# A list scheduler that knows the 64-column form of TensorE matmuls: a four-layer graph network on one NeuronCore

## Chip, cores and metric

The kernel runs on one core of a Trainium2 chip. The metric is the device time of one execution, in microseconds (us). The core has five engines with one instruction queue each: PE (TensorE, matrix multiplication), DVE (VectorE), ACT (ScalarE), POOL (GpSimd) and SP (here it only starts DMA transfers). An engine takes the instructions of its queue in their order; the engines wait for one another by semaphores. PE writes into PSUM, which has eight banks of 512 fp32 values per partition; DVE and ACT read the results from there.

## What is computed

The input is a batch of 64 graphs with 256 nodes and 256 features each, and a 0/1 adjacency matrix per graph. Four residual layers follow one another:

```python
h = relu(layernorm(x)); x = x + gat4(h, adj)        # layer 0: 4 heads of 64, softmax over neighbours, elu
h = relu(layernorm(x)); x = x + relation4(h, adj)   # layer 1: 4 heads of 64, softmax, relu, layernorm per head
h = relu(layernorm(x)); x = x + gat1(h, adj)        # layer 2: 1 head of 256
h = relu(layernorm(x)); x = x + gru3(h, adj)        # layer 3: 3 rounds of h = GRU(A^T (h W_i), h)
```

Layers 0 and 1 end in a product of attention weights and features per head: `alpha[256,256] @ Wh[256,64]`. Layer 3 has, in every round, an aggregation over neighbours and a GRU cell with gates r, z and n.

## The kernel before

**Units.** The graphs are handled in 33 units: one graph, 31 pairs, one graph. `graphs(u, first, nb)` writes down, for one unit, all operations of the four layers (`layer0`, `layer1`, `layer2`, `gru`). It does not run them: every `op(engine, cost, emit, reads, writes, takes)` makes an `_Op` with an estimated cost in ns, and its dependences are taken from the buffers that it reads and writes.

**The scheduler.** `_Schedule.run` then plays the whole program through a simple model of five engines while the kernel is being built, and issues the instructions in the order in which the model starts them. Every operation has a due time, reckoned back from the end that is planned for its unit (one pair per `PACE` = 104000 ns). When an engine of the model falls free, it takes from its heap `able[e]` the operation with the earliest due time whose buffers are to be had (`roomy`). Costs thus do not only describe: **the model's clock decides the order of all five queues, and which slot of a pool (`bank0` to `bank7`, `g0` to `g8` and so on) a buffer gets**, since the free slot with the lowest number is taken when an operation starts. About three units are in flight at a time, so that the matrix products of one unit's GRU stand between the attention of another.

**The 64-column form.** `attend_heads` makes one PE operation out of two heads. Each of its products uses only 64 columns of the array at a time (in the profile: `128*64 128x65`, line 1163); all other products in these layers use all 128. For a pair of graphs the operation has 64 matmuls as the profile counts them. Before the change its cost is

```python
op("pe", pe(944) * len(hs) + 90, emit, [*pts, wh], banks_, takes=[o])
```

that is 1978 ns for two heads of a pair, wherever it stands.

**Names that the prediction uses.** All `vec(...)` calls are recorded by one helper, so they carry line 829; they are told apart by tiles.

- L1163 `bank<-wh,pt`: the attention products (64 columns in layers 0 and 1; full width in layer 2). `pt` are the weights that DVE makes (L1145, and L829 `pt<-pt,cap`). DVE empties the banks by `rs<-bank` (a reciprocal) and `o<-bank,rs`.
- L1032 `bank<-ident,xn`: transposes of the normalised input; ACT copies them by `ht<-bank`.
- L1389 `bank<-ident,ht`: transposes of the new GRU state, in two blocks of 4 matmuls, one for each half `j` of the features. The state's halves are made by the last of a row of DVE operations (`g<-g,ht`, `g<-g,g`, then `ht<-g,g`), which follow ACT's tanh of gate z (`g<-bank,bg`) and of gate n (`g<-g,bg`). From the transposes ACT and DVE make `hl`, the state split into two parts.
- L1361 `bank<-am_r,hl`: the aggregation over neighbours; ACT copies its two banks by `ag<-bank`.
- L1375: the GRU gates, 4 matmuls each: `bank<-ht,whh` needs only the state, `bank<-ag,wc` needs `ag`.
- L1308 `xt<-xt,o` adds the result of layer 1 to `x`; L997 and L998 are statistics of a layer norm, L1006 and L1007 its power on POOL, L1015 its application on ACT.

Of the kernel before, what the change touches and what calls it, by code (L numbers as in the profile page):

```python
# [538 lines left out]
class _Op:  # L539
    __slots__ = (  # L540
        "engine", "cost", "port", "emit", "group", "bufs", "takes", "nbytes", "succs", "waits", "due", "ready",
        "index",
    )


class _Schedule:
# [14 lines left out]
    DMA_RATE = 220.0  # L561
    DMA_AHEAD = 2000
    STRETCH = 3.13
    MARGIN = 800.0

    def __init__(self, tc, pools):
# [8 lines left out]
    def buf(self, cls, shape, dtype=F32, tile=None):  # L575
        return _Buf(cls, shape, dtype, tile)

    def op(self, engine, cost, emit, reads=(), writes=(), takes=(), nbytes=0, port=False):
        o = _Op()
        o.port = port  # L580
        o.engine, o.cost, o.emit, o.group, o.nbytes = engine, cost, emit, self.group, nbytes
        o.succs, o.index, o.ready = [], len(self.ops), 0.0
        deps, o.bufs, o.takes = set(), [], []
        for written, items in ((False, reads), (True, writes)):
            for item in items:
                b, part = item if isinstance(item, tuple) else (item, None)
                if b not in o.bufs:
                    o.bufs.append(b)
                    b.left += 1
                if written and b.tile is None and b not in o.takes:  # L590
                    o.takes.append(b)
                keys = list(b.parts) if part is None else [k for k in (part, None) if k in b.parts]
                for k in keys:
                    writer, readers = b.parts[k]
                    if writer is not None:
                        deps.add(writer)
                    if written:
                        deps.update(readers)
                writer, readers = b.parts.get(part, (None, []))
                if written:  # L600
                    if part is None:
                        b.parts.clear()
                    b.parts[part] = (o.index, [])
                else:
                    b.parts[part] = (writer, readers + [o.index])
        for b in takes:
            if b.tile is None and b not in o.takes:
                o.takes.append(b)
        deps.discard(o.index)
        o.waits = len(deps)  # L610
        for d in deps:
            self.ops[d].succs.append(o)
        self.ops.append(o)
        return o
# [17 lines left out]
                )  # L632
            self.last[i.engine] = i.name

    def enable(self, ops, able):
        for o in ops:
            o.waits -= 1
            if o.waits == 0:
                heapq.heappush(able[o.engine], (o.due, o.index))

    def roomy(self, o):
        need = {}
        for b in o.takes:
            if b.tile is None:
                need[b.cls] = need.get(b.cls, 0) + 1
        return all(len(self.free[c]) >= n for c, n in need.items())
# [9 lines left out]
    def run(self):  # L656
        ops = self.ops
        for o in reversed(ops):
            late = self.end[o.group]
            for s in o.succs:  # L660
                if s.group == o.group or o.group not in self.end or o.group < 0:
                    late = min(late, s.due - self.STRETCH * s.cost - self.MARGIN)
            if o.nbytes:
                late -= self.DMA_LATENCY + o.nbytes / self.DMA_RATE
            o.due = late
        engines = ("pe", "act", "dve", "pool", "sp")
        able = {e: [] for e in engines}
        idle = dict.fromkeys(engines, True)
        events = []
        clock = self.dma_free = self.port_free = 0.0  # L670
        count = 0

        def post(t, kind, o):
            nonlocal count
            count += 1
            heapq.heappush(events, (t, count, kind, o))

        for o in ops:
            if o.waits == 0:
                heapq.heappush(able[o.engine], (o.due, o.index))  # L680
        done = 0
        self.trace = []
        while True:
            for e in engines:
                if not idle[e]:
                    continue
                if e == "sp" and self.dma_free > clock + self.DMA_AHEAD:
                    continue
                held = []
                while able[e]:  # L690
                    item = heapq.heappop(able[e])
                    o = ops[item[1]]
                    if (not o.port or self.port_free <= clock) and self.roomy(o):
                        self.start(o, clock)
                        idle[e] = False
                        free = clock + o.cost - self.OVERLAP[e]
                        post(free, "free", o)
                        if o.port:
                            self.port_free = free
                        break  # L700
                    held.append(item)
                for item in held:
                    heapq.heappush(able[e], item)
            if not events:
                break
            clock = events[0][0]
            while events and events[0][0] == clock:
                _, _, kind, o = heapq.heappop(events)
                if kind == "free":
                    idle[o.engine] = True  # L710
                    if o.nbytes:
                        self.dma_free = max(self.dma_free, clock) + o.nbytes / self.DMA_RATE
                        post(self.dma_free + self.DMA_LATENCY, "done", o)
                        post(max(clock, self.dma_free - self.DMA_AHEAD), "dma", o)
                    else:
                        post(clock + self.OVERLAP[o.engine] + self.HOP[o.engine], "done", o)
                    if o.engine == "pe":
                        self.enable([s for s in o.succs if s.engine == "pe"], able)
                elif kind == "done":
                    done += 1  # L720
                    self.enable([s for s in o.succs if s.engine != "pe" or o.engine != "pe"], able)
                    for b in o.bufs:
                        b.left -= 1
                        if b.left == 0 and b.slot is not None:
                            heapq.heappush(self.free[b.cls], b.slot)
        self.span = clock
        assert done == len(ops), [o.index for o in ops if o.waits][:5]
# [3 lines left out]
def _fast_path(  # L731
# [88 lines left out]
    buf, op = sched.buf, sched.op  # L820
# [4 lines left out]
    def bank(dtype=F32):  # L825
        return buf("bank", [P, S * 4 // mybir.dt.size(dtype)], dtype)
# [149 lines left out]
    def graphs(u, first, nb):  # L976
# [5 lines left out]
        def part_of(fixed):  # L982
            return lambda cost: fixed + (cost - fixed) * nb / 2

        pe, act, dve, pool = part_of(0), part_of(200), part_of(130), part_of(130)
# [172 lines left out]
        def attend(ps, pt, wh, c, h, w, Q):  # L1158
            b, ic = divmod(c, 2)
            for jc in range(2):  # L1160
                for q in range(P // Q):
                    i0 = ic * P + q * Q
                    nc.tensor.matmul(  # L1163
                        ps[q * Q : (q + 1) * Q], lhsT=pt.tile[:, b, jc, i0 : i0 + Q],
                        rhs=wh.tile[:, h, 2 * b + jc, :w], start=(jc == 0), stop=(jc == 1),
                    )

        def attend_heads(o, o_view, pts, wh, hs):

            banks_ = [bank() for _ in hs]  # L1170
            w = E + 1

            def emit():
                for ps, pt, h in zip(banks_, pts, hs):
                    for c in range(C):
                        attend(ps.tile[:, c * w : (c + 1) * w], pt, wh, c, h, w, P // 2)

            op("pe", pe(944) * len(hs) + 90, emit, [*pts, wh], banks_, takes=[o])

            def scaled(ps, h):  # L1180
                rs = buf("rs", [P, C])
                view = lambda: ps.tile[:, : C * w].rearrange("p (c w) -> p c w", c=C)
                vec(nc.vector.reciprocal, 175, lambda: rs.tile, lambda: view()[:, :, E], reads=[ps], writes=[rs])
                vec(nc.vector.tensor_mul, dve(420), lambda: o_view(h), lambda: view()[:, :, :E],
                    lambda: rs.tile[:, :, None].to_broadcast([P, C, E]), reads=[ps, rs], writes=[(o, h)])

            for ps, h in zip(banks_, hs):
                scaled(ps, h)
# [345 lines left out]
```

## Time and profile before

| | |
|---|---|
| median of 3 executions | 3197.43 us (3197.04 to 3197.90) |
| the profiled execution, first to last instruction | 3198.1 us, 0.7 us above that median; nothing outside this span is shown |
| PE busy | 3143.2 us (98%), 18599 matmuls |
| DVE busy | 2321.4 us (73%) |
| ACT busy | 1486.8 us (46%) |
| POOL busy | 897.4 us (28%) |
| DMA | 43 GB/s on average |
| granted PE clock | 0.996 |
| L1163 with 64 columns | 8192 matmuls, 263.7 us busy |

From about 390 us to 2810 us the work repeats itself with every pair: the same order of instructions, one period per pair. Before that the pipeline fills, after it the last units run out. Busy times are sums over an engine's instructions; matmuls are pipelined and their ends are modelled, so the start of the following group is the safer measure of how long a group held PE.

### The profile page before, as it was taken

What the parts mean: (1) busy time and instruction counts of PE and PEld (TensorE: products, weight loads), DVE (VectorE), ACT (ScalarE), POOL (GpSimd) and SP (SyncE); (2) the same over time, 40 slices, a digit from 0 to 9 for tenths busy, and PEclk for the clock granted to TensorE, in tenths of its full rate; (3) what the DMA queues carried; (4) which work ended last, traced back from release to release, by engine and by line L of the source; (5) the groups of instructions that cost most, each with busy time, mean ns of one, the idle gap of its engine ahead of it and who ended that gap; (6) DMA issues with size and microseconds to landing.
All of it is one profiled execution on the core that took longest, in us unless ns stands there. A gap on an engine that the chain in (4) does not pass through costs nothing.

```text
span 3198.1 us, 48707 instructions
## 1 busy us (share of the span) xinstructions
PE 3143.2 (98%) x18599; PEld 1931.9 (60%) x18599; DVE 2321.4 (73%) x5206; ACT 1486.8 (46%) x3128; POOL 897.4 (28%) x907
## 2 busy tenths in 40 slices
PE   7899999999999999999999999999999999999998
PEld 6765656565666655566656566556566556665555
DVE  7777867778767778767678677788677787677753
ACT  5454444454454444454444454544444444544433
POOL 4323332133331233331233321333311333311210
PEclk9999999999999999999999999999999999999999
DMA  4110111101111101111101111111111011101000
GB/s 129 34 49 29 54 54 34 47 31 50 54 54 34 47 31 50 54 47 34 53 28 54 53 36 45 40 41 54 54 34 47 31 50 50 47 23 44 11 16 12
DMA packets 109927, 138.82 MB, mean 43 GB/s; under 512 B 44714, under 2 KB 97524, under 8 KB 102004
## 3 DMA queue, kind: packets, MB, share of 16 engines
q1 hardware_dynamic: 105712, 134.25, 12.8%
q8 instruction: 149, 2.44, 0.3%
q10 hardware_dynamic: 3972, 1.36, 0.2%
q14 instruction: 94, 0.77, 0.1%
HBM read 109.84 MB, written 17.34 MB: 40 GB/s over the span
## 4 chain that ended last, share of the span: by engine, by line
PE 87%; DVE 9%; POOL 2%; ACT 1%; issue 1%; DMA 0%; SPq 0%; ACTq 0%; POOLq 0%; DVEq 0%
PE bank L1375 55%; PE bank L1054 10%; PE bank L1163 10%; PE bank L1361 5%; PE bank L1032 3%; PE bank L1389 2%; DVE pt L1145 2%; DVE g L829 2%; DVE pt L829 1%; POOL mean L1297 1%; POOL o L829 1%; DVE o L829 1%; ACT ht L829 1%; DVE xt L1308 1%; DVE mean L829 1%
## 5 line engine op out<-in xcount | busy, mean ns | idle before, releaser
L1375 PE MATMUL bank<-ag,wc 128*128 128x512 f32 (+1 forms) x2376 | 1063.0, 582 | 0.0
L1375 PE MATMUL bank<-ht,whh 128*128 128x512 f32 (+1 forms) x2376 | 1055.6, 580 | 2.2 <-ACT g L829 1.3
L829 ACT ACTIVATE g<-bank,bg 128x512 f32<-128x512 f32 (+1 forms) x594 | 395.2, 670 | 713.6 <-PE bank L1375 706.6
L1375 PEld LDWEIGHTS bank<-ag,wc 128*128 128x128 f32 x2376 | 441.4, 190 | 459.2 <-issue 441.1
L1375 PEld LDWEIGHTS bank<-ht,whh 128*128 128x128 f32 x2376 | 435.0, 190 | 438.9 <-issue 424.2
L1006 POOL TENSOR_SCALAR mv<-mv 128x4 f32<-128x4 f32 (+1 forms) x132 | 81.9, 621 | 1428.6 <-DVE mv L998 1383.6
L1145 DVE TENSOR_SCALAR pt<-cb,f 128x256 f32<-128x256 f32 x1152 | 416.9, 430 | 6.0 <-ACT cb L1099 5.2
L1163 PEld LDWEIGHTS bank<-wh,pt 128*64 128x64 f32 (+1 forms) x8704 | 345.6, 142 | 94.4 <-issue 76.1
L829 DVE SCALAR_TENSOR_TENSOR g<-g,g 128x512 f32<-128x512 f32 (+1 forms) x396 | 263.3, 670 | 180.4 <-ACT g L829 180.4
L1163 PE MATMUL bank<-wh,pt 128*64 128x65 f32 (+1 forms) x8704 | 382.0, 233 | 9.7 <-DVE pt L829 5.8
L829 DVE TENSOR_TENSOR pt<-pt,cap 128x1024 f32<-128x1024 f32 (+1 forms) x297 | 341.3, 1193 | 0.1
L829 DVE SCALAR_TENSOR_TENSOR g<-bank,g 128x512 f32<-128x512 f32 (+1 forms) x198 | 129.8, 666 | 280.2 <-PE bank L1375 280.0
L829 DVE SCALAR_TENSOR_TENSOR g<-g,ht 128x512 f32<-128x512 f32 (+1 forms) x198 | 136.5, 689 | 172.0 <-ACT g L829 171.6
L1361 PE MATMUL bank<-am_r,hl 128*128 128x256 f32 x1536 | 238.1, 304 | 0.1
L1015 ACT ACTIVATE xn<-xt,mv 128x256 f32<-128x256 f32 x384 | 197.3, 588 | 72.1 <-DVE mv L829 71.9
L1361 PEld LDWEIGHTS bank<-am_r,hl 128*128 128x128 f32 x1536 | 198.2, 189 | 42.5 <-issue 30.6
L829 ACT COPY ag<-bank 128x512 f32<-128x512 f32 (+1 forms) x198 | 113.4, 573 | 233.4 <-PE bank L1361 230.1
L829 ACT ACTIVATE g<-g,bg 128x512 f32<-128x512 f32 (+1 forms) x198 | 137.6, 709 | 161.6 <-DVE g L829 159.4
L997 DVE BATCH_NORM_STATS2 st<-xt 128x6 f32<-128x256 f32 x512 | 208.1, 406 | 6.4 <-DMA xt<-in_x_dram 6.2
L829 ACT COPY ht<-bank 128x512 f32<-128x512 f32 (+1 forms) x264 | 137.8, 573 | 124.0 <-PE bank L1032 123.8
L1136 POOL MEMSET wh<- 128x16 f32 (+3 forms) x99 | 11.8, 120 | 635.5 <-ACT f L1130 635.5
L1007 POOL TENSOR_TENSOR mv<-mv,nhalf 128x4 f32<-128x4 f32 (+1 forms) x132 | 176.0, 1333 | 11.0
(91 smaller groups left out, 3452.2 us busy)
## 6 DMA issues: line engine op xcount, KB each, us to landing
cb<-rd SPq DMA_DIRECT2D x60, 1024.0 KB
xt<-in_x_dram SPq DMA_DIRECT2D x31, 512.0 KB
at<-in_adj_dram SPq DMA_DIRECT2D x31, 512.0 KB
out_dram<-xt SPq DMA_DIRECT2D x31, 512.0 KB
cb<-rd SPq DMA_DIRECT2D x30, 256.0 KB
cap<-cap_n SPq DMA_TRANSPOSE x128
cb<-rd SPq DMA_DIRECT2D x2, 512.0 KB
rd<-row ACTq DMA_DIRECT2D x60, 8.0 KB
```

Of the source, the lines that this page charges most:

```text
L829: emit = lambda: fn(*[a() if callable(a) else a for a in args], **kw)
L997: nc.vector.bn_stats(st.tile[:, c, :], xt.tile[:, c, :])
L1006: nc.gpsimd.tensor_scalar(mv.tile[:, 2, :], mv.tile[:, 1, :], 1e-5, None, op0=OP.add)
L1007: nc.gpsimd.tensor_tensor(mv.tile[:, 2, :], mv.tile[:, 2, :], nhalf[:, :C], op=OP.pow)
L1015: op("act", 610, lambda: nc.scalar.activation(xn.tile[:, c, :], xt.tile[:, c, :], AF.Relu, bias=mv.tile[:, 3, c : c + 1], scale=mv.tile[:, ...
L1032: nc.tensor.transpose(ps.tile[:, c * P : (c + 1) * P], xn.tile[:, c, dc * P : (dc + 1) * P], ident)
L1054: nc.tensor.matmul(ps.tile[:, : heads * W], lhsT=ht.tile[:, dc, c * P : (c + 1) * P], rhs=we[:, dc].rearrange("p h w -> p (h w)"), start=( ...
L1145: nc.vector.tensor_scalar(pt.tile[:, b, jc, :].rearrange("p (i n) -> p i n", n=P), cb.tile[:, h, 2 * b : 2 * b + 2, :], f.tile[:, 1, h, c ...
L1163: nc.tensor.matmul(ps[q * Q : (q + 1) * Q], lhsT=pt.tile[:, b, jc, i0 : i0 + Q], rhs=wh.tile[:, h, 2 * b + jc, :w], start=(jc == 0), stop= ...
L1361: nc.tensor.matmul(ps.tile[:, b * N : (b + 1) * N], lhsT=hl.tile[:, k, 2 * b + sc, :], rhs=am.tile[:, 2 * b + sc, :], start=(k == 0 and sc ...
L1375: nc.tensor.matmul(ps.tile[:, :S], lhsT=w[:, dc, g * P : (g + 1) * P], rhs=v.tile[:, dc, :], start=(first and dc == 0), stop=(last and dc ...
L1389: nc.tensor.transpose(ps.tile[:, c * P : (c + 1) * P], ht.tile[:, j, c * P : (c + 1) * P], ident)
```

## The change

Three things are new in the scheduler, and one line in the kernel.

1. An `_Op` may be `tiled`. Only the operation of `attend_heads` is. Its cost becomes `pe(930) * len(hs)` (1860 ns for a pair), and the model adds `TILING` = 250 ns when such an operation starts after one that is not tiled.
2. PE no longer takes the first of its heap that is roomy, but what `pick` returns: the first by due time, except that after a tiled operation any ready tiled operation goes first.
3. `pick` can also hold a single tiled operation back for `PATIENCE` ns; with `PATIENCE = 0` the comparison `clock - o.ready < 0` never holds.
4. `enable` notes the time at which an operation becomes ready.

No operation is added, left out or altered in what it computes.

```diff
+    TILING = 250
+    PATIENCE = 0
...
-    def enable(self, ops, able):
+    def enable(self, ops, able, clock):
         for o in ops:
             o.waits -= 1
             if o.waits == 0:
+                o.ready = clock
                 heapq.heappush(able[o.engine], (o.due, o.index))
+
+    def pick(self, queue, clock, tiled):
+
+        first = None
+        for item in sorted(queue):
+            o = self.ops[item[1]]
+            if not self.roomy(o):
+                continue
+            if o.tiled and tiled:
+                first = item
+                break
+            if first is None:
+                first = item
+        if first is None:
+            return None
+        o = self.ops[first[1]]
+        if o.tiled and not tiled:
+            mates = sum(self.ops[i].tiled for _, i in queue)
+            if mates < 2 and clock - o.ready < self.PATIENCE:
...
+        queue.remove(first)
+        heapq.heapify(queue)
+        return first
...
+                if e == "pe":
+                    item = self.pick(able[e], clock, tiled)
+                    if item is not None:
+                        o = ops[item[1]]
+                        self.start(o, clock)
+                        idle[e] = False
+                        post(clock + o.cost + (self.TILING if o.tiled and not tiled else 0), "free", o)
+                        tiled = o.tiled
                     continue
...
-            op("pe", pe(944) * len(hs) + 90, emit, [*pts, wh], banks_, takes=[o])
+            op("pe", pe(930) * len(hs), emit, [*pts, wh], banks_, takes=[o], tiled=True)
```

More of the change, by code (lines that the diff above doesn't have):

```diff
@@ L541 @@
         "engine", "cost", "port", "emit", "group", "bufs", "takes", "nbytes", "succs", "waits", "due", "ready",
-        "index",
+        "index", "tiled",
     )
@@ L576, in buf, with op @@
         return _Buf(cls, shape, dtype, tile)
-    def op(self, engine, cost, emit, reads=(), writes=(), takes=(), nbytes=0, port=False):
+    def op(self, engine, cost, emit, reads=(), writes=(), takes=(), nbytes=0, port=False, tiled=False):
         o = _Op()
+        o.tiled = tiled
         o.port = port
@@ L638, in enable @@
             if o.waits == 0:
+                o.ready = clock
                 heapq.heappush(able[o.engine], (o.due, o.index))
+    def pick(self, queue, clock, tiled):
[15 more added lines that the diff above has]
+            if mates < 2 and clock - o.ready < self.PATIENCE:
+                for item in sorted(queue):
+                    p = self.ops[item[1]]
+                    if not p.tiled and self.roomy(p):
+                        first = item
+                        break
+        queue.remove(first)
+        heapq.heapify(queue)
+        return first
     def roomy(self, o):
@@ L671, in run @@
         count = 0
+        tiled = False
         def post(t, kind, o):
@@ L687, in run @@
                 if e == "sp" and self.dma_free > clock + self.DMA_AHEAD:
+                    continue
+                if e == "pe":
[6 more added lines that the diff above has]
+                        tiled = o.tiled
                     continue
@@ L717, in run @@
                     if o.engine == "pe":
-                        self.enable([s for s in o.succs if s.engine == "pe"], able)
+                        self.enable([s for s in o.succs if s.engine == "pe"], able, clock)
                 elif kind == "done":
                     done += 1
-                    self.enable([s for s in o.succs if s.engine != "pe" or o.engine != "pe"], able)
+                    self.enable([s for s in o.succs if s.engine != "pe" or o.engine != "pe"], able, clock)
                     for b in o.bufs:
```

## Prediction

> **What bounds the kernel now.** I read the page's busy times first, then its chain of work that ended last, then the list of PE's waits, then one pair's period on PE and DVE in order of time. "The built order" below is the order of instructions, buffer slots and semaphore waits that the two programs have once built; it holds no times.
>
> ```profile
> PE 3143.2 (98%) x18599; PEld 1931.9 (60%) x18599; DVE 2321.4 (73%) x5206; ACT 1486.8 (46%) x3128; POOL 897.4 (28%) x907
> ...
> PE 87%; DVE 9%; POOL 2%; ACT 1%; issue 1%; DMA 0%; SPq 0%; ACTq 0%; POOLq 0%; DVEq 0%
> ```
>
> ```profile
> PE bank L1389 <- DVE ht L829: 8.6, 14, 1.8
> ...
> PE bank L1389 <- ACT ht L829: 3.2, 18, 0.3
> ```
>
> PE is the bound. A change of order can gain only where PE stands still or changes form. 9% of the chain runs over DVE, so in some stretch DVE is as late as PE. The waits (us in total, times, longest) name it: 32 times PE waited at L1389 for the new GRU state. In order of time, 25 of these 32 come once per period, 96.92 us apart, from 393.66 to 2719.66 us; the other 7 lie after 2940 us. In the repeated part PE has no other idle entry. One of the 25, first PE, then DVE (start, duration, what):
>
> ```profile
> 1454.11 3.96 PE L1163 MATMUL bank<-wh,pt 128*64 128x65 f32 x128
> 1458.00 1.09 PE L1032 MATMUL bank<-ident,xn 128*128 128x128 f32 x8
> 1458.93 0.65 PE L1389 MATMUL bank<-ident,ht 128*128 128x128 f32 x4
> 1459.75 0.63 PE L1389 MATMUL bank<-ident,ht 128*128 128x128 f32 x4 [0.17 <-DVE ht L829]
> ...
> 1495.73 0.60 PE L1389 MATMUL bank<-ident,ht 128*128 128x128 f32 x4
> 1496.17 1.88 PE L1375 MATMUL bank<-ht,whh 128*128 128x512 f32 x4
> ```
>
> ```profile
> 1454.52 0.67 DVE L829 SCALAR_TENSOR_TENSOR g<-g,ht 128x512 f32<-128x512 f32 x1
> 1455.12 0.68 DVE L1308 TENSOR_TENSOR xt<-xt,o 128x512 f32<-128x512 f32 x1
> ...
> 1456.32 0.41 DVE L997 BATCH_NORM_STATS2 st<-xt 128x6 f32<-128x256 f32 x1
> 1456.77 0.18 DVE L998 BATCH_NORM_AGGREGATE mv<-st 128x2 f32<-128x6 f32 x1
> ...
> 1458.21 0.66 DVE L829 SCALAR_TENSOR_TENSOR ht<-g,g 128x512 f32<-128x512 f32 x1
> 1458.79 0.24 DVE L829 RECIPROCAL rs<-bank 128x4 f32<-128x4 f32 x2
> 1458.95 0.66 DVE L829 SCALAR_TENSOR_TENSOR ht<-g,g 128x512 f32<-128x512 f32 x1
> ```
>
> A block of four L1389 normally holds PE for 1496.17 - 1495.73 = 0.44 us. Here the second block starts 1459.75 - 1458.93 = 0.82 us after the first: **0.38 us is lost in each period** (the 0.17 in brackets is less, since part of it lies under the modelled end of the last matmul). The second `ht` ends at 1459.61, and PE goes on 0.14 us later. Ahead of that `ht` DVE ran L1308 and one pair L997/L998, which this state does not need.
>
> **What the Trainium skill says.** "TensorE: Matmul & The Clock Gate", Step-by-step: what each phase is for: matmuls stay in program order, only weight loads are pulled ahead; so a late L1389 holds back everything behind it. The trace agrees: L1375, needing nothing new, starts only at 1460.22. "TensorEngine Tiling (Array Packing)", Key Properties: changing the tiling mode drains TensorE. The trace shows a small price (below). "PSUM — Partial Sum Buffer", PSUM bank collisions raise a hardware error: guard PSUM by bank. So the slot matters: as built before, the second L1389 block reuses `bank0` of the L1032 transposes, and waits for ACT's copy out of it as well as for `ht`.
>
> **The change part by part.** *Grouping.* In the built orders the runs of 64-column products on PE go from 99 to 97. In every period both have three: two lone operations with one gate between them, and one run of two. The two that vanish lie at the start and at the last unit. The chain of waits prices one: a lone L1163 x64 takes 2.02 us, x128 takes 3.89, so 64 more cost 1.87, and entering 0.15; the gate after it takes 1.91 instead of 1.72 (0.19). Two fewer: 2 x 0.34 = 0.7 us gained. The charge of 250 ns is close to this, but is paid in the model alone.
>
> *Order in the period.* The new costs (2110 instead of 1978 ns for a lone operation, 3970 instead of 3956 for two) shift the model's clock. In the built order the period on PE keeps its 83 rows, and one moves: gate h (`ht,whh`) of the first half goes ahead of the two L1361. PE does no more and no less. On DVE, L1308 and the L997/L998 pair go behind both `ht` and the four `o<-bank,rs`. On ACT, the tanh of the second z goes ahead of the two tanh of n. The second L1389 block gets `bank7`, which nobody holds: its wait for ACT's copy is gone.
>
> When is the second `ht` ready now? DVE and ACT durations are those of this period; starts follow one another at 0.59 to 0.61 us for the 512-wide ones. PE ends the second z gate at 1454.11, so ACT has z at about 1454.90, n of the halves at 1455.5 and 1456.1. DVE: `g<-g,ht` at 1454.52 and 1455.12, `g<-g,g` at 1455.72 and 1456.32, two reciprocals at 1456.92, first `ht` 1457.08 to 1457.74. The next two reciprocals need the last of L1163, which ends at about 1458.07: they run to 1458.3, the second `ht` to about 1458.9. PE wants it at 1458.93 + 0.44 = 1459.37, with the 0.14 us of hand-over: 0.3 us to spare. Only PE itself is ahead of it then. Gain 0.38 us x 25 = **9.5 us**.
>
> *What is late next.* (a) `hl` needs DVE after the moved L1308: first `hl` at about 1461.4, second at 1463.25; PE now reaches L1361 at 1459.81 + 2 x 1.72 = 1463.25 and needs the second at about 1464.4. (b) `ag`: one gate, no longer two, stands between L1361 and the first `ag,wc`. ACT's second copy ended at 1464.03 + 0.59 = 1464.62, 0.63 us after L1361 (the chain ends that at 1463.99); there are now 1.72 us, 1.1 to spare. (c) The L1015 rows wait for the later statistics: `mv` at about 1468.75 instead of 1468.3, and ACT has one more tanh first; the four rows end at about 1471.4, PE asks at 1472.0. (d) The first gate now also waits for `o<-bank,rs` to free `bank1`: 1459.3 against 1459.8. All hold, none by much. DMA and SP: SP's order is unchanged; ACT's and POOL's moved rows have idle time around them.
>
> Near the end the old trace shows one unit with the new order on PE:
>
> ```profile
> 2913.02 3.60 PE L1375 MATMUL bank<-ht,whh 128*128 128x512 f32 x8
> 2916.06 2.46 PE L1361 MATMUL bank<-am_r,hl 128*128 128x256 f32 x16
> 2918.35 1.88 PE L1375 MATMUL bank<-ht,whh 128*128 128x512 f32 x4
> 2920.07 1.88 PE L1375 MATMUL bank<-ag,wc 128*128 128x512 f32 x4
> ```
>
> The `ag,wc` gate starts 1.72 us after its forerunner: no stall with one gate between. That speaks for (b).
>
> *Start and end.* Between 38 and 233 us PE's idle entries add to 15.3 us, after 2940 us to 10.0 us. Some thirty rows of PE change places there, DVE and ACT more. No row of the old trace prices the new mixture; neither end excludes a gain or a loss. I take 0, with 3 us either way: a fifth of the start's idle time.
>
> Sum: 3198.1 - 9.5 - 0.7 = 3187.9 us of span; the median lies 0.7 below the profiled span: 3187.2 us.
>
> **Rivals.** *The stall stays in part, or start and end eat the gain.* For: 0.3 us to spare hangs on ACT's and DVE's hand-overs, and in 17 of the 25 periods the trace names ACT, not DVE, as the last releaser. If 0.25 of the 0.38 us stays, 25 x 0.13 = 3.3 us and the 0.7 are gained: 3193.5 us, within 0.2% (6.4 us, about what a measurement of this kernel can tell from no change). *The change does not do what it says*: grouping indeed hardly occurs; were the moved rows worth nothing too, 3196.8 us. *Slower by a new wait.* The place is (b): the first `ag,wc` gate. ACT has the two `hl` copies and two exponentials ahead of `ag`; if its second copy comes d us after L1361's end, PE loses d - 1.72 in every period, and the whole gain of 10.2 us is used up when that passes 0.41 us, at d = 2.1. At d = 2.6 the loss is 25 x 0.88 = 22 us: 3209 us. Against it: 0.63 now, ACT busy 46%, and the unit at 2913 us.
>
> **How the numbers follow.** The stall gone and nothing late: 0.70, 3187.2 us, its own range 3182 to 3191. Part of it or nothing: 0.19, 3191 to 3197.5. A new wait: 0.11, above 3204. Faster by over 0.2% means below 3191.0: 0.70; the same 0.19; slower 0.11. The range runs from 3181, both ends gained and 3 us more, to 3197.5, which leaves out the new wait and little else.
>
> **What would show it.** Right: no idle entry at L1389 between 400 and 2700 us, a period of about 96.54 us, L1308 behind `ht` on DVE. Wrong: an idle entry at L1375 `ag,wc`, L1361 or L1032 in every period; a period of 96.9 us; or a difference that lies before 390 or after 2810 us.

## The result, and the profile after

The changed kernel takes **3218.43 us** (median of 5, 3218.26 to 3219.55), the kernel before beside it on the same chip 3197.43 us (3196.61 to 3199.21). The ratio is 1.0065, 95% interval 1.0053 to 1.0077: **slower by 21 us**. The prediction was 3187.2 us, faster. The profiled execution of the changed kernel spans 3216.5 us, 18.4 more than before, at the same clock of 0.996.

In the changed kernel all lines from the scheduler on stand 41 further down: L1389 is now L1430, L1361 L1402, L1375 L1416, L1163 L1204, L1032 L1073, L1308 L1349, the helper L829 is L870. The page, first the busy times and the shares of the chain, then the longest of PE's waits:

```profile
PE 3143.2 (98%) x18599; PEld 1931.7 (60%) x18599; DVE 2352.7 (73%) x5206; ACT 1477.8 (46%) x3128; POOL 934.3 (29%) x907
...
PE 71%; DVE 16%; POOL 11%; issue 2%; ACT 1%; DMA 0%; POOLq 0%; SPq 0%; ACTq 0%; DVEq 0%
```

```profile
PE bank L1430 <- DVE ht L870: 31.7, 31, 1.8
```

PE's busy time is unchanged to the tenth of a microsecond. Nothing was added to PE; it waits. The wait for `ht` at this line has grown from 11.8 us (8.6 that name DVE and 3.2 that name ACT) to 32.0 us (31.7 and 0.3), and **the chain now goes 11% over POOL, where it was 2%**. DVE and POOL are busy for 31 and 37 us more, with the same number of instructions.

In order of time, one period on PE: the transposes of the *last* GRU round's state, and a little later those of the *first* round of the next unit, which is the place that the prediction was about.

```profile
1446.12 0.60 PE L1430 MATMUL bank<-ident,ht 128*128 128x128 f32 x4
1447.70 0.63 PE L1430 MATMUL bank<-ident,ht 128*128 128x128 f32 x4 [0.98 <-DVE ht L870]
1448.16 1.88 PE L1416 MATMUL bank<-ht,whh 128*128 128x512 f32 x4
...
1470.24 1.15 PE L1430 MATMUL bank<-ident,ht 128*128 128x128 f32 x8
1471.23 3.60 PE L1416 MATMUL bank<-ht,whh 128*128 128x512 f32 x8
```

At the first round both blocks now take 1471.23 - 1470.24 = 0.99 us; before it was 0.82 + 0.47 = 1.29. So 0.30 of the predicted 0.38 us are gained. But at the last round, where before there was no wait, the second block starts 1.58 us after the first and not 0.44: **1.14 us are lost**. The entry stands there 25 times, once per period, from 372 to 2719 us.

I measure the period from one run of 128 products of 64 columns to the next. Before it is 96.92 us ((2713.99 - 388.00) / 24), after 97.77 ((2736.47 - 389.87) / 24). The 0.85 us are 1.14 - 0.30 within 0.01, and 25 x 0.85 = 21 us.

Why is this `ht` late? First DVE of the changed kernel, then POOL, in the same period:

```profile
1432.06 1.57 DVE L870 SCALAR_TENSOR_TENSOR g<-g,g 128x512 f32<-128x512 f32 x1
1433.55 0.74 DVE L870 TENSOR_TENSOR o<-bank,rs 128x256 f32<-128x256 f32 x2
...
1444.04 0.68 DVE L870 SCALAR_TENSOR_TENSOR g<-g,g 128x512 f32<-128x512 f32 x1
1446.26 0.69 DVE L870 TENSOR_TENSOR o<-o,mean 128x512 f32<-128x512 f32 x1 [1.55 <-POOL mean L1338]
1446.87 0.68 DVE L870 SCALAR_TENSOR_TENSOR ht<-g,g 128x512 f32<-128x512 f32 x1
...
1451.99 1.75 DVE L1349 TENSOR_TENSOR xt<-xt,o 128x512 f32<-128x512 f32 x1 [0.56 <-POOL o L870]
...
1470.03 0.65 DVE L870 SCALAR_TENSOR_TENSOR ht<-g,g 128x512 f32<-128x512 f32 x1
```

```profile
1429.88 1.66 POOL L870 TENSOR_TENSOR o<-o,bias_b 128x512 f32<-128x512 f32 x1 [1.54 <-DVE o L870]
1431.80 1.27 POOL L870 TENSOR_TENSOR hl<-hn,hl 128x512 fp32r<-128x512 f32 x1 [0.27 <-ACT hl L1387]
1434.37 1.27 POOL L870 TENSOR_TENSOR o<-o,bias_b 128x512 f32<-128x512 f32 x1 [1.29 <-DVE o L870]
...
1443.41 0.76 POOL L1337 TENSOR_SCALAR mean<-mean 128x8 f32<-128x8 f32 x1
1444.26 1.97 POOL L1338 TENSOR_TENSOR mean<-mean,nhalf 128x8 f32<-128x8 f32 x1
...
1449.02 1.26 POOL L870 TENSOR_TENSOR o<-o,gamma_b 128x512 f32<-128x512 f32 x1
```

And the rows of the kernel before that answer to them, DVE and POOL:

```profile
1424.11 0.68 DVE L829 SCALAR_TENSOR_TENSOR g<-g,g 128x512 f32<-128x512 f32 x1
...
1434.08 0.68 DVE L829 SCALAR_TENSOR_TENSOR ht<-g,g 128x512 f32<-128x512 f32 x1
1434.68 0.68 DVE L829 TENSOR_TENSOR o<-o,mean 128x512 f32<-128x512 f32 x1
...
1439.79 1.74 DVE L1308 TENSOR_TENSOR xt<-xt,o 128x512 f32<-128x512 f32 x1 [0.56 <-POOL o L829]
```

```profile
1419.74 1.65 POOL L829 TENSOR_TENSOR o<-o,bias_b 128x512 f32<-128x512 f32 x1 [1.54 <-DVE o L829]
1421.67 1.27 POOL L829 TENSOR_TENSOR hl<-hn,hl 128x512 fp32r<-128x512 f32 x1 [0.28 <-ACT hl L1346]
1422.90 1.27 POOL L829 TENSOR_TENSOR o<-o,bias_b 128x512 f32<-128x512 f32 x1
...
1431.84 0.57 POOL L1296 TENSOR_SCALAR mean<-mean 128x8 f32<-128x8 f32 x1 [0.35 <-DVE mean L829]
...
1436.82 1.27 POOL L829 TENSOR_TENSOR o<-o,gamma_b 128x512 f32<-128x512 f32 x1
```

`o<-o,mean` belongs to the layer norm of layer 1 in another unit: POOL adds a bias, DVE makes the mean, POOL makes the power (L1337, L1338), DVE multiplies by it, POOL multiplies by gamma and adds beta, DVE adds the result to `x` (L1349). In what follows (r+1)*n is one row of the GRU on DVE, the one that multiplies the value of gate n by r + 1. Two rows have changed places on DVE. **First**, the second `ht` stands behind `o<-o,mean`, which waits 1.55 us for POOL. **Second**, (r+1)*n of the last round (`g<-g,g` at 1432.06) stands ahead of the two `o<-bank,rs`, lasts 1.57 us there instead of 0.68, and POOL, which waits for `o<-bank,rs`, stands idle for 1.29 us. Measured from POOL's `hl`, its L1337 begins at 11.61 us and not at 10.17, that is 1.44 us later. The two L1337 rows then take 0.76 and 0.70 us instead of 0.57 and 0.26, so that POOL's gamma row begins 19.14 us after the first `o<-o,bias_b` and not 17.08: **2.06 us late**. Against that, the block on DVE that follows, from L1349 to the end of the second `ht` of the next unit's first round, takes 18.69 us and not 19.82, because L1349 of the second half and a pair of statistics now stand behind it.

### The profile page after: what moved, and what is told of

Same layout as the page of the kernel before. It is cut to its first block, busy times and chain, and to the rows that moved or that the text cites. A ratio compares the mean times of both kernels' runs of the same rounds, so it can differ in the third digit from the quotient of the medians.

```text
span 3216.5 us, 48911 instructions
## 1 busy us (share of the span) xinstructions
PE 3143.2 (98%) x18599; PEld 1931.7 (60%) x18599; DVE 2352.7 (73%) x5206; ACT 1477.8 (46%) x3128; POOL 934.3 (29%) x907
## 4 chain that ended last, share of the span: by engine, by line
PE 71%; DVE 16%; POOL 11%; issue 2%; ACT 1%; DMA 0%; POOLq 0%; SPq 0%; ACTq 0%; DVEq 0%
PE bank L1416 43%; PE bank L1095 10%; PE bank L1204 8%; DVE pt L1186 5%; PE bank L1402 3%; POOL cap_n L1271 3%; PE bank L1073 3%; PE bank L1430 2%; DVE g L870 2%; DVE pt L870 2%; DVE o L870 2%; POOL mv L1048 2%; POOL mean L1338 2%; POOL mv L1047 2%; DVE st L1038 1%
## 5 line engine op out<-in xcount | busy, mean ns | idle before, releaser
L1416 PE MATMUL bank<-ag,wc 128*128 128x512 f32 (+1 forms) x2376 | 1062.9, 582 | 0.0
L1416 PE MATMUL bank<-ht,whh 128*128 128x512 f32 (+1 forms) x2376 | 1054.1, 580 | 1.1 <-ACT ht L870 0.9
L870 ACT ACTIVATE g<-bank,bg 128x512 f32<-128x512 f32 (+1 forms) x594 | 395.9, 672 | 805.9 <-PE bank L1416 797.7
L1416 PEld LDWEIGHTS bank<-ag,wc 128*128 128x128 f32 x2376 | 441.5, 190 | 459.0 <-issue 446.8
L1416 PEld LDWEIGHTS bank<-ht,whh 128*128 128x128 f32 x2376 | 433.8, 190 | 437.0 <-issue 409.4
L870 DVE SCALAR_TENSOR_TENSOR g<-g,g 128x512 f32<-128x512 f32 (+1 forms) x396 | 284.9, 730 | 190.9 <-ACT g L870 190.9
L1204 PEld LDWEIGHTS bank<-wh,pt 128*64 128x64 f32 (+1 forms) x8704 | 346.4, 142 | 98.1 <-issue 78.5
L1204 PE MATMUL bank<-wh,pt 128*64 128x65 f32 (+1 forms) x8704 | 382.0, 233 | 14.6 <-DVE o L870 9.7
L870 DVE TENSOR_TENSOR pt<-pt,cap 128x1024 f32<-128x1024 f32 (+1 forms) x297 | 338.7, 1182 | 0.1
L870 DVE SCALAR_TENSOR_TENSOR g<-bank,g 128x512 f32<-128x512 f32 (+1 forms) x198 | 129.5, 665 | 246.5 <-PE bank L1416 246.1
L870 DVE SCALAR_TENSOR_TENSOR g<-g,ht 128x512 f32<-128x512 f32 (+1 forms) x198 | 130.0, 666 | 171.7 <-ACT g L870 171.3
L1402 PE MATMUL bank<-am_r,hl 128*128 128x256 f32 x1536 | 238.6, 304 | 0.1
L870 ACT COPY ag<-bank 128x512 f32<-128x512 f32 (+1 forms) x198 | 112.8, 571 | 265.5 <-PE bank L1402 265.1
L1402 PEld LDWEIGHTS bank<-am_r,hl 128*128 128x128 f32 x1536 | 198.3, 189 | 42.9 <-issue 30.3
L870 ACT ACTIVATE g<-g,bg 128x512 f32<-128x512 f32 (+1 forms) x198 | 137.5, 709 | 168.7 <-DVE g L870 168.5
L870 ACT COPY ht<-bank 128x512 f32<-128x512 f32 (+1 forms) x264 | 137.4, 571 | 119.4 <-PE bank L1073 119.4
L1048 POOL TENSOR_TENSOR mv<-mv,nhalf 128x4 f32<-128x4 f32 (+1 forms) x132 | 185.9, 1408 | 11.0
```

What stands on the lines that cost most here:

```text
L870: emit = lambda: fn(*[a() if callable(a) else a for a in args], **kw)
L1048: nc.gpsimd.tensor_tensor(mv.tile[:, 2, :], mv.tile[:, 2, :], nhalf[:, :C], op=OP.pow)
L1204: nc.tensor.matmul(ps[q * Q : (q + 1) * Q], lhsT=pt.tile[:, b, jc, i0 : i0 + Q], rhs=wh.tile[:, h, 2 * b + jc, :w], start=(jc == 0), stop= ...
L1402: nc.tensor.matmul(ps.tile[:, b * N : (b + 1) * N], lhsT=hl.tile[:, k, 2 * b + sc, :], rhs=am.tile[:, 2 * b + sc, :], start=(k == 0 and sc ...
L1416: nc.tensor.matmul(ps.tile[:, :S], lhsT=w[:, dc, g * P : (g + 1) * P], rhs=v.tile[:, dc, :], start=(first and dc == 0), stop=(last and dc ...
```

## The experiments

The moves below were made in the list of instructions that the scheduler puts out, in every period; nothing else changes. "Before" in their ratios is the kernel before, run beside them. Their code for the moves shifts lines: L959 is the helper, L1525 or L1528 the state's transposes, L1163 here the transposes of the normalised input, L1510 or L1513 the gates, L1499 the aggregation, L1294 the attention products, L1429 and L1430 (L1431 and L1432 in the last ones) POOL's power of the mean. The diffs show the order on the engine. Most differences are below 1%; the ratios say which are clear of noise.

Two theories went in. Theory 1: each stall is a matter of its own place; `ht` waits because it stands behind a row that waits for POOL. Theory 2, made after the first four runs: there is also a loop, PE's 64-column products, DVE `o<-bank,rs`, POOL's layer norm, DVE's unbroken block from L1349 to `ht`, PE's first round, which has nothing to spare; what POOL is late by comes back there.

What PE lost, per period: the first round's site is the sum of the `ident,xn` and `ident,ht` groups over 1.80 us (0.93 + 0.87), the last round's the `ident,ht` groups over 0.87. Without waits a period would be 96.92 - 0.42 = 96.50 us. The last column is the way round the loop of theory 2: from the start of the first lone 64-column run on PE to the end of the second `ht` of the first round that follows it (before: 1415.03 to 1459.61), as the median of 18 periods.

| kernel | median us | ratio to before (95%) | period us | lost, first round | lost, last round | loop us |
|---|---|---|---|---|---|---|
| before | 3197.43 | | 96.92 | 0.42 | 0 | 44.59 |
| after | 3218.43 | 1.0053 to 1.0077 | 97.77 | 0.12 | 1.16 | 45.50 |
| a_ht_first | 3211.06 | 1.0027 to 1.0055 | 97.45 | 0.95 | 0 | 45.19 |
| a_rn_late | 3197.54 | 0.9989 to 1.0006 | 96.93 | 0.10 | 0.31 | 44.66 |
| a_ht_rn | 3191.00 | 0.9966 to 0.9985 | 96.62 | 0.12 | 0 | 44.35 |
| b_om_first | 3210.98 | 1.0025 to 1.0053 | 97.35 | 0.85 | 0 | 45.00 |
| b_rn_early | 3228.51 | 1.0077 to 1.0110 | 98.06 | 1.22 | 0 | 45.71 |
| b_both | 3242.13 | 1.0120 to 1.0154 | 98.51 | 1.37 | 0.30 | 46.18 |

(The last two lose 0.33 us more at the last round's aggregation, whose group takes 2.30 instead of 1.97 us.)

**The two moves, undone one by one in the changed kernel.** `a_ht_first`:

```diff
 g<-g,g
+ht<-g,g
 o<-o,mean
-ht<-g,g
```

> The changed kernel, with one row moved on DVE in every period: the second `ht` of the last GRU round goes ahead of `o<-o,mean` of the other unit. Theory (the loss is that `ht` stands behind a DVE row that waits for POOL): the new stall of 1.14 us at the last round's L1430 goes in all 25 periods, 3218.4 - 25 x 1.14 = 3189.9 us, between 3187 and 3193. Rival 'PE itself is slower in its new order (the 64-column form or the moved gate)': stays at 3218. Rival 'POOL's rows are late and whoever waits for them holds PE anyway': stays above 3210, with the wait at another row.

`a_rn_late`:

```diff
-g<-g,g          # (r+1)*n, second half
 o<-bank,rs
 o<-bank,rs
+g<-g,g
```

> The changed kernel, with DVE's (r+1)*n of the last round's second half (`g<-g,g` 128x512) moved behind the two `o<-bank,rs` that POOL's bias addition waits for; `ht` stays behind `o<-o,mean`. Theory (the order on DVE costs something only because POOL is 1.4 us late at that point): POOL's L1337 starts some 1.1 us earlier, `o<-o,mean` at about 1.2 us earlier, the stall falls from 1.14 us to 0.2 or less: 3190 to 3195 us. Rival 'the order on DVE is enough by itself': stays at 3218. I also expect the row `g<-g,g`, 1.57 us in the changed kernel, to take about 0.7 us again.

In `a_ht_first` the stall at the last round is gone, as theory 1 said, and yet only 7.4 of the expected 28 us were gained. PE of that kernel, first round:

```profile
1464.85 1.09 PE L1163 MATMUL bank<-ident,xn 128*128 128x128 f32 x8
1466.37 1.39 PE L1525 MATMUL bank<-ident,ht 128*128 128x128 f32 x8 [0.43 <-DVE ht L959]
1467.60 3.61 PE L1510 MATMUL bank<-ht,whh 128*128 128x512 f32 x8
```

From 1464.85 to 1467.60 PE spends 2.75 us on what takes 1.80: **the stall went to the first round**. There too PE waits for an `ht`, but no row that waits for POOL stands just ahead of it. This was a miss of theory 1; it is what the last rival of that expectation said, above 3210 us with the wait at another row. In `a_rn_late` POOL's second `o<-o,bias_b` again begins without a wait, and 20.9 us come back: 3197.54 us, above the expected 3190 to 3195. Of the stall 0.31 us are left, more than the 0.2 expected, and (r+1)*n takes 0.85 us, not 0.7.

**The two moves, made in the kernel before.** `b_om_first` moves `ht` behind `o<-o,mean`; `b_both` moves (r+1)*n ahead of `o<-bank,rs` as well; PE's order is that of before in both.

```diff
-ht<-g,g
 o<-o,mean
+ht<-g,g
```

> The kernel before, with the second `ht` of the last round moved behind `o<-o,mean` on DVE, as the changed kernel has it; POOL's rows are not later. Theory (order and POOL's lateness are both needed): `ht` ends at about 0.4 us before PE wants it, no new stall, 3197.4 us within 2 us. Rival 'the order is enough': 3197.4 + 25 x 1.1 = 3225 us.

> The kernel before, with both moves: the second `ht` of the last round behind `o<-o,mean`, and (r+1)*n of that round's second half ahead of the two `o<-bank,rs`. PE's order is that of before. Theory: the stall of the changed kernel appears, some 0.9 to 1.1 us in each of 25 periods: 3219 to 3226 us. Rival 'PE's new order or the 64-column form is what costs': 3197 to 3200 us.

`b_om_first` missed both expectations: no stall at the last round, and still 0.43 us more per period. The trace puts it on POOL. After POOL's first L1430 its next row, and the DVE row beside it:

```profile
1441.52 0.70 POOL L1429 TENSOR_SCALAR mean<-mean 128x8 f32<-128x8 f32 x1
```

```profile
1441.46 0.69 DVE L959 TENSOR_TENSOR o<-o,mean 128x512 f32<-128x512 f32 x1 [0.34 <-POOL mean L1430]
```

This POOL row takes 0.26 us in the kernel before. Here DVE's `o<-o,mean`, released by POOL itself, begins 0.06 us earlier and holds it up for 0.44 us, and the period grows by 0.43. `b_both` shows that the two DVE moves by themselves cost 44 us, with PE's order and 64-column runs as before: I had expected 22 to 29 us, since I had counted the last round only.

**POOL's lateness alone.** `b_rn_early` leaves `ht` where it was:

```diff
+g<-g,g          # (r+1)*n, second half
 o<-bank,rs
 o<-bank,rs
...
-g<-g,g
```

> The kernel before, with one row moved on DVE: (r+1)*n of the last round's second half ahead of the two `o<-bank,rs`; `ht` stays ahead of `o<-o,mean`. Theory 1 (POOL's lateness reaches PE only through an `ht` that stands behind a row waiting for POOL): 3197 to 3199 us. Theory 2 (the loop PE, DVE `o<-bank,rs`, POOL's layer norm, DVE L1308 to `ht`, PE has no slack left in the kernel before; every 1 us that POOL starts later comes back at the first round's `ht`): a stall ahead of the first `ht` block of the first round, as with both moves together, period 98.2 to 98.5 us, 3230 to 3240 us.

Theory 1 fails by 30 us. Theory 2 has the place right, with 3228.51 us and a period of 98.06 us just below its ranges. (r+1)*n takes 1.56 us, POOL's `o<-o,bias_b` waits 1.29 us, POOL's multiplication by gamma begins 1.14 us later than before, counted from the first `o<-o,bias_b`, and the period is 1.14 us longer. **What POOL is late by, the period is longer by, one for one.** The 0.43 of `b_om_first` and this 1.14 add up to 1.57; `b_both` has 98.51 - 96.92 = 1.59. The table shows the same for all eight kernels: in each the loop differs from that of before by what the period differs, within 0.07 us (after: 0.91 and 0.85; `a_ht_first`: 0.60 and 0.53; `b_both`: 1.59 and 1.59).

**Both repairs.** `a_ht_rn` makes both of the first two moves in the changed kernel.

> The changed kernel with both repairs: `ht` of the last round ahead of `o<-o,mean`, and (r+1)*n behind the two `o<-bank,rs`. Theory 1 (each stall is a matter of its own place): no stall left, period 96.6 us, 3189 us. Theory 2 (the loop over POOL): the 0.31 us that are still lost at the last round with the second repair alone come back at the first round, since POOL's second mean ends 0.9 us later than in the kernel before; period 96.8 to 96.95 us, 3194 to 3198 us.

Theory 1's number was nearer: 3191.00 us, no stall at the last round. It is the loop all the same: POOL's gamma row still comes 0.89 us later than in the kernel before, and the DVE block is 1.13 us shorter, which my range for theory 2 had left out. The loop is 0.24 us shorter and the period 0.30. This version is faster than both kernels, than before by 0.15 to 0.34%.

**Which part of the diff did it.** `cost_only` leaves out the preference for the 64-column form:

```diff
-            if o.tiled and tiled:
+            if False:
                 first = item
```

> The changed kernel with the preference for ready operations of the 64-column form taken out of the scheduler's choice; the new costs and the charge for entering the form stay. If the costs alone made the new order: as the changed kernel, 3216 to 3220 us, with the same stall at the last round's L1430. If the grouping did: as before, 3197 us.

3219.60 us, ratio 1.0050 to 1.0084, with the same stall (1.16 us at the last round) and the same loop (45.50 us): the new costs, the charge for entering among them, made the order, not the preference that groups.

**The predicted gain by itself.** `b_onto_late` and `b_onto_last` make, in the kernel before, only the DVE move from which the prediction drew its gain.

```diff
-xt<-xt,o        # L1308
-st<-xt, mv<-st
 ...             # g<-g,ht and so on
 ht<-g,g         # second half
+xt<-xt,o        # b_onto_late: here;
+st<-xt, mv<-st  # b_onto_last: behind the o<-bank,rs
 o<-bank,rs      # four times
```

> The kernel before, with L1308 of the second half and the first pair of statistics moved behind both `ht` of the first round and nothing else: the part of the change that the prediction counted as its gain. POOL starts as early as before. Both theories: the 0.38 us stall at the first round goes, 3197.4 - 25 x 0.3 to 0.38 = 3188 to 3190 us. If DVE's block ahead of `ht` were not what PE waits for there, 3197.

> The kernel before, with L1308 of the second half and the first pair of statistics moved behind both `ht` of the first round and behind the four `o<-bank,rs` too, as the changed kernel has them (the run before this one put them between, and PE's next gate waited 0.5 us for `o<-bank,rs`). POOL as before. Expected of the loop theory: the loop gets about 1.1 us shorter, the stall at the first round goes, period 96.55 to 96.65 us, 3189 to 3191 us. If the predicted gain did not exist by itself, 3197.

Neither gains: 3210.34 us (ratio 1.0025 to 1.0050) and 3200.07 us (0.9996 to 1.0014), both outside what I expected. The stall at the `ht` blocks is gone, with the second block still in `bank0`; so ACT's copy out of that bank, which the profile names in 17 of the 25 periods, was not what PE waited for. PE of the two, after these blocks:

```profile
1464.69 1.55 PE L1510 MATMUL bank<-ht,whh 128*128 128x512 f32 x3 [0.53 <-DVE o L959]
```

```profile
1461.89 0.80 PE L1499 MATMUL bank<-am_r,hl 128*128 128x256 f32 x2
1462.86 1.93 PE L1499 MATMUL bank<-am_r,hl 128*128 128x256 f32 x14 [0.17 <-DVE hl L959]
```

In the first the next gate waits for `o<-bank,rs`, in the second the aggregation waits for `hl`, which DVE makes after L1308; the loop itself is 0.73 us shorter than before in both (43.86 and 43.85 us). So the DVE move alone gains nothing. What lets it pay in the new order should be gate h ahead of the two aggregations, which gives `hl` 1.72 us more: there PE has no wait at the aggregation. No run makes these two moves alone.

**The price of the 64-column form.** `g_ahead2` and `g_behind` start from `a_ht_rn` and do in 20 periods what the change is named for: the gate between the two lone 64-column runs goes ahead of both, or behind both.

```diff
+bank<-ag,wc     # g_ahead2
 bank<-wh,pt x64
-bank<-ag,wc
 bank<-wh,pt x64
```

> The changed kernel with both repairs (3191.0 us), and on PE the gate between the two lone 64-column runs moved ahead of the first, in 20 periods, so that they become one run of 128; on DVE the two reciprocals of the first run go behind (r+1)*n, since they are ready later. Price of entering the form as the prediction has it, 0.34 us: 20 x 0.34 = 6.8 us gained, 3184 us, if the loop over POOL has 0.1 us to spare. If entering costs nothing: 3191 us. If POOL comes later by more than the loop has to spare: above 3191 us, with a stall at the first round's `ht`.

> As the run before, but the gate goes behind the second lone run, and DVE's order stays. The second run's `pt` is ready only some 0.3 us after PE gets there: of the 0.34 us some 0.04 are left, 3190 us, with an idle entry of 0.2 to 0.4 us at L1294 in 20 periods. If the later gate makes (r+1)*n and POOL late by more than the loop has to spare, above 3192 us.

PE of `a_ht_rn`, then of `g_ahead2`:

```profile
1409.16 3.60 PE L1510 MATMUL bank<-ht,whh 128*128 128x512 f32 x8
1412.69 2.09 PE L1294 MATMUL bank<-wh,pt 128*64 128x65 f32 x64
1414.70 1.98 PE L1510 MATMUL bank<-ag,wc 128*128 128x512 f32 x4
1416.62 2.09 PE L1294 MATMUL bank<-wh,pt 128*64 128x65 f32 x64
1418.64 1.98 PE L1510 MATMUL bank<-ag,wc 128*128 128x512 f32 x4
1420.46 1.02 PE L1510 MATMUL bank<-ht,whh 128*128 128x512 f32 x2
```

```profile
1409.88 3.60 PE L1513 MATMUL bank<-ht,whh 128*128 128x512 f32 x8
1413.32 1.88 PE L1513 MATMUL bank<-ag,wc 128*128 128x512 f32 x4
1415.13 3.96 PE L1294 MATMUL bank<-wh,pt 128*64 128x65 f32 x128
1419.02 1.98 PE L1513 MATMUL bank<-ag,wc 128*128 128x512 f32 x4
1420.84 0.59 PE L1513 MATMUL bank<-ht,whh 128*128 128x512 f32 x1
```

The same work takes 11.30 and 10.96 us: **one entry less saves 0.34 us**, entering and leaving together, as the prediction priced it (in the Trainium skill, "TensorEngine Tiling (Array Packing)", Key Properties, says that the switch drains TensorE). Yet `g_ahead2` gains nothing: 3193.76 us (0.9980 to 0.9994). Its interval overlaps that of `a_ht_rn`, but in the traces its period is longer, 96.75 us against 96.62, and the first round's site loses 0.60 us instead of 0.12. The first run's result comes later on DVE, and POOL's gamma row begins 2.21 us after PE's transposes of the last round (1434.02) instead of 1.72: 0.49 us later. The loop takes back somewhat more than the form gave. `g_behind` runs in 3201.21 us (1.0001 to 1.0019), with an idle entry of 0.47 us at the first round and none at L1294. Its first expectation failed and its second came: above 3192 us, with POOL's gamma row 0.54 us later after the first `o<-o,bias_b` than in `a_ht_rn`.

**What stretches (r+1)*n.** `a_hl_late` changes POOL's order only:

```diff
-hl<-hn,hl
 o<-o,bias_b     # second half
+hl<-hn,hl
```

> The changed kernel, with one row moved on POOL: the first `hl<-hn,hl` goes behind the second `o<-o,bias_b`, so that no POOL row of 512 runs beside DVE's (r+1)*n; DVE's order is that of the changed kernel. If the 1.57 us of `g<-g,g` come from POOL's `hl` running beside it: it takes 0.7 us, the second `o<-o,bias_b` starts 0.9 us earlier, and since the 1.27 us of `hl` now follow it, L1337 starts 0.2 to 0.4 us later and the period is longer by that: 3222 to 3228 us. If they come from DVE's own order: 1.57 us stay.

3230.98 us (1.0085 to 1.0119), above the expected 3222 to 3228; the period is 98.25 us, 0.48 more than the changed kernel, and POOL's gamma row comes 0.47 us later after the first `o<-o,bias_b`. The DVE row that the run was for:

```profile
1437.29 0.66 DVE L959 SCALAR_TENSOR_TENSOR g<-g,g 128x512 f32<-128x512 f32 x1
```

0.66 us in place of 1.57, at the same place on DVE: POOL's `hl` beside it was the cause. In the changed kernel `hl` ends at 1433.07 and the DVE row 0.56 us after that.

## Why the prediction was wrong

**The step that failed is "What is late next", and with it its last sentence, "ACT's and POOL's moved rows have idle time around them".** The list (a) to (d) looked at the first round and at the buffers around it. It left out the second `ht` of the last round, which the new order puts behind `o<-o,mean`, and it left out (r+1)*n, which goes ahead of `o<-bank,rs`. "Order in the period" does not name these two rows at all. POOL is busy for 28% of the span; but in the kernel before it has hardly a gap between the first `o<-o,bias_b` and the last row of the layer norm, and both ends of that stretch hang on DVE. A low share of the whole span said nothing on that stretch. The runs show in its place a loop over POOL: its gamma row comes 2.06 us later, the DVE block behind it is 1.13 us shorter, and the period is 0.85 us longer where the prediction had it 0.38 us shorter.

**How the lateness reaches PE.** The loop sets how much PE loses in a period, the order of the rows sets where. In the changed kernel most of it, 1.16 us, is lost at the last round, since an `ht` stands there behind a row that waits for POOL. With that closed (`a_ht_first`) the loop is only 0.31 us shorter, and PE loses 0.95 us at the first round instead. With (r+1)*n put back as well (`a_ht_rn`), 0.12 us are lost in all. The place where PE waits was thus not where the time came from.

**The gain term** was right in kind and mis-sized: 0.30 us per period and not 0.38. The prediction let DVE's rows ahead of the first round's `ht` begin as early as before: `g<-g,ht` 0.41 us after PE's run of 128 products. In the changed kernel it is 1.29 us (1466.72 - 1465.43), since DVE's block hangs on POOL. The 0.3 us to spare are gone with that: the second `ht` ends 1.37 us after PE begins the `ident,xn` group, where some 0.9 were predicted. In the two `b_onto` runs, with POOL on time, it ends 0.88 us after it. The term was also taken to hang on the DVE move, with PE's move as a side issue; the `b_onto` runs show that the DVE move alone gains nothing.

**What held.** PE's work is unchanged (3143.2 us). The price of an entry, 0.34 us. Points (a) to (d): between 400 and 2720 us the changed kernel has no idle entry on PE but those at L1430. (a) and (d) were the right places to look at: they are where the two `b_onto` runs stall. The rival that ended on the slower side had the right sign and the wrong place, (b). One reading proves less than it says: L1375 at 1460.22 reads both halves of the new state, so it waits for the same `ht` as L1389, and its late start is no evidence for the order on PE.

**Start and end** were taken as 0 with 3 us either way. In the two profiled executions 24 periods cost 20.6 us more. From the last run of 128 products to the end the changed kernel takes 3216.5 - 2930.23 = 286.3 us, before it was 3198.1 - 2907.73 = 290.4: 4.1 us gained. At the start it is 389.87 - 388.00 = 1.9 us behind, one new stall included. That makes the 18.4 us between the two spans; the medians lie 21.0 us apart, and since executions of the kernel before differ by up to 3 us, the 4.1 us may in part be the one that was profiled.

## To carry to other kernels

When a scheduler's costs change, list every row that changes places on every engine, and ask for each what it waits for and who stands behind it. Of the two rows that mattered here one moved by a single place, and the other, (r+1)*n ahead of `o<-bank,rs`, cost more. An engine that is busy for 28% can lie on a loop without slack: follow the loop from engine to engine in order of time before calling its rows covered. In such a loop a saving on the bounding engine is worth only what the loop has to spare: taking a real 0.34 us per period from PE made the period 0.13 us longer. And the place where the busiest engine waits need not be where the time comes from: undoing the row that PE waited behind gave back 7.4 of 21 us.

## What the runs showed of the hardware

In these runs a DVE row that reads two tensors of SBUF (the on-chip memory) and a POOL row that reads SBUF beside it do not share, one is held up by the other: (r+1)*n takes 1.57 us beside POOL's `hl` and 0.66 without it, and the other way about POOL's mean row takes 0.70 us beside `o<-o,mean` and 0.26 without it. The page "SBUF — State Buffer" of the Trainium skill, section SBUF: two separate sides, says so: the port pair of the two engines is locked for a whole instruction, and whoever starts first keeps it. The trace agrees (the row that began second ended second, by 0.56 and by 0.07 us), and shows how the cost goes on: in the profile the wait has no entry of its own, it only makes a row longer, and it falls on whatever the longer row holds back.

The scheduler's model has this port: operations marked `port=True` are not started while another one holds it, so in the model `hl` and (r+1)*n never run side by side. On the chip `hl` began 0.26 us before (r+1)*n (1431.80 and 1432.06). The power of the mean on POOL isn't marked at all. An order that is right by the model's clock met the lock on the chip.
